# Four pre-activation layers on one core: the last image's layer 3 in another order, with one step for all norms' roots, lent buffers and evictions on either engine

## The chip, the cores and the metric

The kernel runs on one core of a Trainium2 chip. The metric is the device time of one execution in microseconds, the median of three runs. The core has TensorE (PE, matmul; PEld, its weight loads), VectorE (DVE), ScalarE (ACT), GpSimd (POOL, unused here but for a few memsets) and SyncE (SP), whose queue issues all DMAs.

## What is computed

Eight images of 32 channels and 256x256 pixels go through four layers. Each layer is `x = x + conv(gn(x))`, with a group norm over pairs of channels that needs the whole image first.

```
x = x + L0(gn(x))   # 1x1 conv; then each channel convolved with its own 5x5 pooled map
x = x + L1(gn(x))   # quantised: out = -sum |patch - w| over 32 channels x 3x3, for 32 outputs
x = x + L2(gn(x))   # 3x3 conv plus bias
x = x + L3(gn(x))   # on 8x8 windows:
#   y = layernorm(windows)
#   a = kan1(y in one 16-wide order);  d = kan2(y in another);  e = kan3(y, 32 channels)
#   out = kan4(a + d + e) + windows
# kan(v): b_k = exp(-((layernorm(v) - g_k) / denom)**2), k = 0..7
#         result = sum_k W_k b_k + W silu(v)
```

## The kernel before, in words

**Tiles.** An image of layer 3 is cut in eight units (NCH = 8) of 128 partitions x 2048 float32 (F). A unit's matmuls are 32x32 blocks: a *group* (mm16, L593) is 16 program matmuls of 512 columns, which the trace shows as 32, and it fills the PSUM tile psB (128x2048) or, in halves of eight, the tile psA (128x1024).

**Planner.** Nothing is issued in the order of the code. Every step is a task with an engine, an assumed duration, buffers and a rank (`Plan.add`). `Plan.run` simulates the four engines with these durations, picks the ready task of lowest rank whose buffers are free, and writes down the order; the engines then run this fixed order. `LAT` is the assumed hand-over from one engine to another. Buffers have kinds: `bas` (3 places for kan bases), `si` (3), `rs` (2, roots), `dv` (3 places of 128x4128 bf16, distances of layer 1), `psA`, `psB` (one each), `psV` (2, variances), and `sb`, pieces of a large arena.

**Layer 1** is not made of tasks but of *passes* (`Pass`), which fill what is left: VectorE, or in halves ScalarE, makes a clipped difference (L977, L979) into a `dv` buffer (in the first image a `bas` one also), and TensorE gathers it into psA with eight matmuls (L999). A pass ends with an eviction of psA (L1046). There are 16 passes for an image and 36 distances for each.

**Images overlap.** While layer 1 of image b runs, layer 0 of image b+1 and layers 2 and 3 of image b-1 run beside it. When the last pass of image 7 is over, only the rest of layer 3 of image 6 and layers 2 and 3 of image 7 are left, with nothing beside them: this is what is called the last image here.

**Layer 3.** A *kan* is, for a unit: scale the centred values by the roots (matmul L1264, multiply L1272 on VectorE), eight bases (a square on ScalarE, L1368, or, once layer 1 is over, a product on VectorE instead, L1374; then an exp, L1381, on ScalarE), eight groups into psB, a group of the silu, others that are added, and one eviction (L1447, or L1449 for the last kan). The kans are numbered 0 to 3 in the code, 0 being kan1 of the reference; 4 is the first layernorm. Before a kan stands `variance`: centre with a matmul (L593 into psB, in the last image in two halves into psA), evict (L1219), square (L1224), sum with a matmul into psV (L1232). `roots` makes Ln and Exp (L1245, L1249) of a psV. Exp and Ln share one table of ScalarE, silu (L1313, L1479) needs another; a change costs a table load (L1554). The planner keeps table stretches in the order in which they were added.

Results move between the layouts by DMA: y, yd and their silus are stored and read again (prepare, L1324 and L1326; L1345, L1348), so are the results oa and od of kans 0 and 1 (L1463), which kan 2 adds (load2: four DMAs for oa, L1405, sixteen for od, L1409).

**The order of a turn** is written in the last loop of `stage3`. Turn t runs kan 0 of unit t, kan 3 of unit t-1, kan 1 and kan 2 of unit t, and prepares unit t+1 and the first norm of unit t+2. Roots are made at three places of a turn, "A" (kan 0 and the next first norm), "B" (kans 1 and 3) and "C" (kan 2).

Of the kernel before, what the change touches and what calls it, by code (L numbers as in the profile page):

```python
# [89 lines left out]
class Buf:  # L90


    def __init__(self, kind, words=0):
        self.kind, self.words = kind, words
        self.writers, self.readers = [], []
        self.tile = None
        self.left, self.first, self.at, self.taken, self.base = 0, None, None, False, kind == "bas"
        self.spill = False
# [6 lines left out]
class Plan:  # L105
# [4 lines left out]
    LAT = {"PE": 0.15, "DVE": 0.12, "ACT": 0.25, "SP": 2.0}  # L110

    def __init__(self, room):
# [9 lines left out]
        self.first_pass = 0  # L122
# [40 lines left out]
    def fits(self, need, spare):  # L163
# [3 lines left out]
        for b in need:  # L167
            if b.kind in ("dv", "bas") and b.spill:
                b.kind = "dv" if self.places["dv"] else "bas"
            if b.base:  # L170
                b.kind = "bas" if self.places["bas"] else "sb"
                spare = BASE_SPARE
            if b.kind in self.places and not self.places[b.kind]:
# [17 lines left out]
    def bases_full(self):  # L191
        return not self.places["bas"] and sum(n for _, n in self.free["sb"]) < F + BASE_SPARE
# [35 lines left out]
    def run(self):  # L228
# [23 lines left out]
        while left or any(not p.done for p in self.passes):  # L252
            moved = True
            while moved:
                moved = False
                for e in engines:
# [3 lines left out]
                    if best is None:  # L260
                        for t in ready[e]:
# [4 lines left out]
                            if t.eng != e and not all(p.done for p in self.passes[self.first_pass :]):  # L266
# [5 lines left out]
                        if best is not None:  # L272
                            ready[best.eng].remove(best)
                            if best.other:
                                ready[best.other[0]].remove(best)
                                if best.eng != e:
                                    self.sets[best.stretch][1] -= 1
# [8 lines left out]
                    t.load = None  # L286
                    if t.table in (LN_EXP, SILU):
# [55 lines left out]
    def slack(self, p):  # L343
        return p.b == 0 or self.now - self.idle > IDLE

# [19 lines left out]
class Pass:  # L365
# [38 lines left out]
    def on_pe(self, plan, urgent):  # L404
# [5 lines left out]
        if self.sums and len(self.queue) < URGENT and (late or not (urgent or self.queue)):  # L410
            t, us, bufs, n = self.sums.pop(0), 0.53, [], 1
            fn = lambda: self.parts.gather(self, None, None, t)
        elif self.queue and (len(self.queue) >= URGENT or not urgent):
            o, t, d = self.queue.pop(0)
            us, bufs, n = 0.53, [d], 1
# [21 lines left out]
def kernel(  # L437
# [142 lines left out]
    def sb(b, n=None):  # L580
        return b.tile[:, : n or b.words] if b.tile is not None else arena[:, b.at : b.at + (n or b.words)]
# [588 lines left out]
    def stage3(b, norm, x3buf, rank, span):  # L1170
# [26 lines left out]
        stat = {(k, t): (Buf("psV"), Buf("rs")) for t in range(-2, U + 2) for k in "ABC"}  # L1197
# [6 lines left out]
        def parts():  # L1204

            if b < nb - 1:
# [3 lines left out]
        def variance(n, t, cen, bias, rk, src, sq=None):  # L1210
# [3 lines left out]
            for p, ps, i, us in parts():  # L1214
                at = slice(i * FS, (i + (2 if us < 1 else 4)) * FS)
                plan.add("PE", 0.85 + 0.2 * us, lambda ps=ps, i=i: cen(ps(), i), r=src, w=[p], acc=[c], rank=rk, spare=SPARE)
                plan.add(
# [6 lines left out]
            plan.add("ACT", 1.9, lambda: nc.scalar.activation(sb(sq), sb(c), AF.Square), r=[c], w=[sq], rank=rk)  # L1224
            v = stat[t][0]
# [52 lines left out]
        def front(t, after, rk):  # L1278
# [6 lines left out]
            st[t]["c4"] = variance(4, ("A", t - 1), cen, cb, rk, [xt, sm["cenf"], sm["c3"]], xt)  # L1285

        def middle(t):

            rk = turn(t - 1.0)
            y, yd = st[t]["c4"], Buf("sb", F)  # L1290
            scale(4, ("A", t - 1), y, rk)
# [17 lines left out]
        def silus(t):  # L1309
            rk = turn(t - 0.9)  # L1310
# [363 lines left out]
```

## Time and profile before

| what | us |
|---|---|
| median of three runs | 15973.13 (15972.1 to 15999.17) |
| the profiled execution | 15969.78 |
| its span, first to last instruction | 15967.3 |
| last eviction of a layer-1 pass (L1046) starts | 14601.76 |
| first and last eviction of layer 2, last image (L1145) start | 14725.80, 14837.18 |
| first eviction of layer 3, last image (L1219) starts | 14851.12 |
| evictions of kan 2 (L1447), units 1 and 6, last image, start | 15158.52, 15801.13 |
| last eviction (L1449) starts | 15956.57 |

Over the whole span PE is busy 12928.0 us (81%), DVE 13454.6 (84%), ACT 12386.4 (78%), and POOL 16.7. The kernel has no one bound: until 14601.8 VectorE and ScalarE are both nearly full, after that the engines wait for each other. The table's last lines cut out five whole turns of layer 3, from one eviction of kan 2 to the fifth after it. A busy PE in the profile is not a PE at its peak, since matmuls overlap.

### The profile page before, as it was taken

How to read it: one execution, taken by the hardware profiler on the slowest of the kernel's cores; microseconds unless marked ns; L12 is line 12 of the kernel's file. 1: busy time of each engine (PE TensorE's matmuls, PEld its weight loads, DVE VectorE, ACT ScalarE, POOL GpSimd, SP SyncE). 2: the span in 40 equal slices, each digit the busy share in tenths (PEclk: the TensorE clock that was granted, in tenths of full speed). 3: DMA queues.
4: the chain of work that ended last, by engine and by line, in shares of the span. 5: the costliest groups of instructions: out<-in, count | busy, mean ns of one | idle time of the engine just before them, and what ended most of it. 6: DMA issues, size and time to landing. Idle time of an engine off the chain costs nothing. (4 is left out here: it accounts for less than half of the span.)

```text
span 15967.3 us, 560619 instructions
## 1 busy us (share of the span) xinstructions
PE 12928.0 (81%) x260296; PEld 4325.8 (27%) x260296; DVE 13454.6 (84%) x12544; ACT 12386.4 (78%) x6843; POOL 16.7 (0%) x25
## 2 busy tenths in 40 slices
PE   5889887987887888788887888788878888877666
PEld 4333322222332222232222222222222222222222
DVE  2889889898878889888999988999898989897465
ACT  0899749678658766866888987899779987997687
POOL 0000000000000000000000000000000000000000
PEclk8989899999999999899999999899999999998777
DMA  4332446445445444643554454444544454444554
GB/s 117 78 96 54 105 113 169 109 107 153 130 101 152 126 112 120 166 106 105 152 132 123 126 134 122 122 123 127 127 126 126 126 122 138 116 132 114 144 154 130
DMA packets 1192870, 1970.85 MB, mean 123 GB/s; under 512 B 362752, under 2 KB 878848, under 8 KB 1092224
## 3 DMA queue, kind: packets, MB, share of 16 engines
q1 hardware_dynamic: 1190528, 1934.98, 46.1%
q8 instruction: 2036, 33.36, 0.9%
q14 instruction: 306, 2.51, 0.1%
HBM read 1162.83 MB, written 771.75 MB: 121 GB/s over the span
## 5 line engine op out<-in xcount | busy, mean ns | idle before, releaser
L977 DVE TENSOR_SCALAR dv<-qh,w1q 128x4128 bf16<-128x4128 bf16 (+1 forms) x8831 | 10521.9, 1248 | 1376.3 <-PE psA L999 1319.3
L999 PE MATMUL psA<-dv,sel_b 128*32 128x512 bf16 x71240 | 5434.0, 405 | 1339.6 <-DVE dv L977 1054.2
L999 PEld LDWEIGHTS <-sel_b 128*32 128x32 bf16 x82944 | 2053.9, 97 | 6792.6 <-issue 5786.5
L1368 ACT ACTIVATE bas<-arena,kb 128x2048 f32<-128x2048 f32 x1386 | 2762.3, 1993 | 408.3 <-DVE arena L1272 262.9
L1381 ACT ACTIVATE bas<-bas 128x2048 f32<-128x2048 f32 x1386 | 2653.1, 1914 | 39.0
L979 ACT ACTIVATE dv<-qh,w1n 128x2064 bf16<-128x2064 bf16 x827 | 1628.6, 2009 | 1126.8 <-PE psA L999 1035.3
L593 PE MATMUL psB<-bas,tl 32*32 32x512 f32 x48416 | 1955.5, 652 | 491.1 <-ACT bas L1381 247.6
L873 PE MATMUL psB<-arena,wt 32*32 32x512 f32 (+1 forms) x51040 | 1848.5, 607 | 99.5 <-issue 61.4
L593 PE MATMUL psB<-arena,tl 32*32 32x512 f32 x22496 | 909.4, 621 | 161.7 <-ACT si L1449 46.1
L593 PEld LDWEIGHTS psB<-bas,tl 32*32 32x32 f32 x48416 | 535.2, 107 | 1384.3 <-ACT bas L1381 518.8
L873 PEld LDWEIGHTS psB<-arena,wt 32*32 32x32 f32 x51040 | 651.2, 104 | 778.1 <-issue 607.1
L1368 ACT ACTIVATE arena<-arena,kb 128x2048 f32<-128x2048 f32 x410 | 816.1, 1991 | 0.0
L1381 ACT ACTIVATE arena<-arena 128x2048 f32<-128x2048 f32 x410 | 785.0, 1915 | 12.3
L624 DVE BATCH_NORM_STATS2 tiny<-arena 128x6 f32<-128x512 f32 x768 | 473.5, 679 | 351.8 <-ACT arena L906 246.0
L999 PE MATMUL psA<-qh,sel_b 128*32 128x512 bf16 x9216 | 672.2, 393 | 92.3 <-DMA qh<-q 77.9
L1447 ACT ACTIVATE si<-psB,cols_sb 128x2048 f32<-128x2048 f32 x192 | 377.4, 1966 | 453.3 <-PE psB L593 369.9
L1272 DVE TENSOR_TENSOR arena<-psB,arena 128x2048 f32<-128x2048 f32 x280 | 640.5, 2287 | 86.2 <-PE psB L1264 79.2
L593 PE MATMUL psB<-si,tl 32*32 32x512 f32 x14080 | 630.6, 624 | 48.8 <-ACT si L1447 19.5
L1129 PE MATMUL psB<-arena,tl 32*32 32x512 f32 (+3 forms) x16384 | 626.6, 608 | 14.7 <-issue 14.4
L1224 ACT ACTIVATE arena<-arena 128x2048 f32<-128x2048 f32 x320 | 612.7, 1915 | 15.7 <-DMA x<-arena 5.8
L1264 PE MATMUL psB<-rs,tl 32*32 32x512 f32 x8960 | 338.9, 630 | 222.5 <-DVE arena L1272 128.2
L906 ACT ACTIVATE arena<-psB,cc 128x2048 f32<-128x2048 f32 x64 | 125.7, 1964 | 493.2 <-PE psB L894 493.2
(151 smaller groups left out, 7686.6 us busy)
## 6 DMA issues: line engine op xcount, KB each, us to landing
arena<-x SPq DMA_DIRECT2D x128, 1024.0 KB
arena<-y SPq DMA_DIRECT2D x128, 1024.0 KB
si<-sy SPq DMA_DIRECT2D x512, 256.0 KB
arena<-in_x_dram SPq DMA_DIRECT2D x240, 384.0 KB
arena<-in_x_dram SPq DMA_DIRECT2D x256, 256.0 KB
x<-arena SPq DMA_DIRECT2D x256, 256.0 KB
xr<-x SPq DMA_DIRECT2D x512, 128.0 KB
x<-xr SPq DMA_DIRECT2D x512, 128.0 KB
```

What stands on the lines that cost most here:

```text
L593: nc.tensor.matmul(o[j * C : (j + 1) * C, i - first, :], w_, src(rows, i, j), start=start, stop=stop)
L624: nc.vector.bn_stats(self.stats[:, at + i, :], a[:, i * 512 : (i + 1) * 512])
L873: nc.tensor.matmul(o[:, lo - 2 * j : hi - 2 * j, c0:c1], wt[rows, t, :], d[rows, lo + dy + 2 : hi + dy + 2, c0 + dx : c1 + dx], start=firs ...
L977: nc.vector.tensor_scalar(dst, src, w1q[:, at : at + 1], 0.0, ALU.subtract, ALU.max)
L979: nc.scalar.activation(dst, src, AF.Relu, bias=w1n[:, at : at + 1])
L999: nc.tensor.matmul(psA[j * C : (j + 1) * C, i, :], sel_b[:, n, :], src[:, at : at + 2, t % 3 : t % 3 + W], **flags,)
L1129: nc.tensor.matmul(o[:, lo - 2 * j : hi - 2 * j, c0:c1], (wc if t == 4 else tl[:, W2T + t, :])[rows], d[rows, lo + dy + 1 : hi + dy + 1, c ...
L1224: plan.add("ACT", 1.9, lambda: nc.scalar.activation(sb(sq), sb(c), AF.Square), r=[c], w=[sq], rank=rk)
L1272: lambda ps=ps, at=at: nc.vector.tensor_tensor(sb(c)[:, at], ps().rearrange("p s f -> p (s f)"), sb(c)[:, at], ALU.mult),
L1368: lambda k=k, bas=bas: nc.scalar.activation(sb(bas), sb(rb), AF.Square, bias=kb[:, n, k : k + 1]),
L1381: lambda k=k, bas=bas, square=square: nc.scalar.activation(sb(bas), sb(bas), AF.Exp, scale=-1.0, bias=0.0 if square.eng == "ACT" else kbsq ...
L1447: nc.scalar.activation(sb(o), psB.rearrange("p s f -> p (s f)"), AF.Identity, bias=obias)
```

## The change

The durations that the planner assumes are changed: LAT, the gather (0.53 to 0.49), and 0.05 more for TensorE when it changes between a gather and another task. The rest works only in the last image, or once all passes are over (`over()`):

- bases may lie in `dv` places, and `si` tiles too (a new flag `side`), when their own places are full;
- the half evictions of `variance` and its square may run on VectorE instead of ScalarE, whichever is free first;
- the turn is `alone(t)` instead of `beside(t)` (the old order): one psV and one pair of roots for four norms of the turn, for unit t's kans 1 and 2, unit t+1's kan 0, unit t+2's first norm and unit t-1's kan 3. Kans run in the order 1, 2, 3, 0, and units run one turn further ahead;
- kan 2's loads of oa and od wait for its first exp instead of its fifth.

```diff
-    LAT = {"PE": 0.15, "DVE": 0.12, "ACT": 0.25, "SP": 2.0}
+    LAT = {"PE": 0.2, "DVE": 0.15, "ACT": 0.3, "SP": 2.0}
...
             if b.base:
-                b.kind = "bas" if self.places["bas"] else "sb"
+                b.kind = "bas" if self.places["bas"] else "dv" if self.over() and self.places["dv"] else "sb"
                 spare = BASE_SPARE
+            if b.side:
+                b.kind = "si" if self.places["si"] or not self.over() else "dv" if self.places["dv"] else "sb"
...
-                            if t.eng != e and not all(p.done for p in self.passes[self.first_pass :]):
+                            if t.eng != e and not self.over():
                                 continue
...
+                    if e == "PE":
+                        us += 0.05 * ((t.n is None) != self.filling)
+                        self.filling = t.n is None
...
+    def over(self):
+        return all(p.done for p in self.passes[self.first_pass :])
...
-            t, us, bufs, n = self.sums.pop(0), 0.53, [], 1
+            t, us, bufs, n = self.sums.pop(0), 0.49, [], 1
...
-            us, bufs, n = 0.53, [d], 1
+            us, bufs, n = 0.49, [d], 1
...
-                plan.add(
+                evict = plan.add(
                     "ACT", 0.15 + 1.8 * us,
...
-            plan.add("ACT", 1.9, lambda: nc.scalar.activation(sb(sq), sb(c), AF.Square), r=[c], w=[sq], rank=rk)
-            v = stat[t][0]
+                evict.other = "DVE", 0.15 + 2.1 * us, lambda ps=ps, at=at: nc.vector.tensor_scalar(
+                    sb(c)[:, at], ps().rearrange("p s f -> p (s f)"), shift, None, ALU.add
+                )
+            square = plan.add("ACT", 1.9, lambda: nc.scalar.activation(sb(sq), sb(c), AF.Square), r=[c], w=[sq], rank=rk)
+            square.other = "DVE", 2.3, lambda: nc.vector.tensor_tensor(sb(sq), sb(c), sb(c), ALU.mult)
+            v = stat.setdefault(t, (Buf("psV"), Buf("rs")))[0]
...
-                        "SP", 2.0 if name == "oa" else 8.0, load2, r=[db], w=[a], rank=rk, after=exps[4:5], spare=F,
+                        "SP", 2.0 if name == "oa" else 8.0, load2, r=[db], w=[a], rank=rk, after=exps[(0 if last else 4) :][:1], spare=F,
...
+        def alone(t):
+
+            now, nxt, old = 0 <= t < U, 0 <= t + 1 < U, 1 <= t
+            if now:
+                prepare(1, t, t, turn(t - 0.6), exp0(2, t - 1))
+            if t + 2 < U:
+                front(t + 2, t, turn(t - 0.5), exp0(2, t - 1) or (st[t + 1]["y"].writers if nxt else []))
+            if now:
+                prepare(2, t, t, turn(t - 0.4), exp0(2, t - 1))
+            if nxt:
+                prepare(0, t + 1, t, turn(t - 0.2), exp0(3, t - 2))
+            if old:
+                prepare(3, t - 1, t, turn(t - 0.3), [])
+            roots(t, turn(t))
+            if now:
+                kan(1, t, t, turn(t + 0.05))
+            if t + 2 < U:
+                middle(t + 2, t, turn(t))
+            if old:
+                silu_z(t - 1, turn(t + 0.1))
+            if t + 2 < U:
+                silus(t + 2, turn(t + 0.1))
+            if now:
+                kan(2, t, t, turn(t + 0.25))
+            if old:
+                kan(3, t - 1, t, turn(t + 0.5))
+            if nxt:
+                kan(0, t + 1, t, turn(t + 0.75))
+
+        for t in range(-2, U + 1):
+            (alone if last else beside)(t)
```

`prepare`, `front`, `middle`, `silus` and `silu_z` take the turn's psV and the rank as arguments now; what they do is the same. `exp0(n, t)` is the first exp of kan n of unit t.

## The prediction, made before the changed kernel was run

> **What bounds the kernel now.** I read the busy time by stretches first, then the costliest groups, and then, for the last image's layer 3, ScalarE's and TensorE's order of time. The columns of the stretch table are the stretch and its length, then busy us (with instructions) of PE, PEld, DVE, ACT and POOL, then the granted clock, the DMA share and GB/s.
>
> ```profile
> 12000.00:14000.00 2000.00, 1643.85 (x30910) 509.08 (x30908) 1806.72 (x1520) 1757.74 (x975) 3.89 (x2) 0.92 0.48 127
> ...
> 14601.80:14725.80 124.00, 79.00 (x1686) 34.43 (x1686) 70.00 (x61) 87.82 (x48) 0.00 (x0) 0.78 0.51 120
> ...
> 14851.10:14939.60 88.50, 40.53 (x504) 7.75 (x504) 26.06 (x16) 42.16 (x29) 0.00 (x0) 0.60 0.38 131
> 14939.60:15158.50 218.90, 145.67 (x2520) 49.57 (x2520) 134.74 (x69) 186.11 (x116) 0.00 (x0) 0.76 0.56 150
> 15158.50:15801.10 642.60, 432.19 (x7968) 154.42 (x7968) 401.38 (x203) 536.70 (x324) 0.00 (x0) 0.77 0.56 155
> 15801.10:15967.30 166.20, 102.01 (x1856) 28.65 (x1856) 73.50 (x36) 112.18 (x67) 0.00 (x0) 0.76 0.36 96
> ```
>
> Two kernels stand here one behind the other. Up to 14601.8, where the last gather of layer 1 is evicted, VectorE makes distances and is 90% busy, ScalarE 88%. After it only the last image is left, and no engine is full: between 15158.5 and 15801.1 five whole turns of layer 3 take 128.5 us each, of which ScalarE works 536.7/5 = 107.3 and stands idle 21.2, while VectorE works 80.3.
>
> ```profile
> L977 DVE TENSOR_SCALAR dv<-qh,w1q 128x4128 bf16<-128x4128 bf16 (+1 forms) x8831 | 10521.9, 1248 | 1376.3 <-PE psA L999 1319.3
> ```
>
> Nearly all of VectorE's idle time in the long part is a wait for TensorE to give back one of three distance buffers. The idle time of a turn looks like this:
>
> ```profile
> 15047.43 1.02 ACT L1219 ACTIVATE arena<-psA 128x1024 f32<-128x1024 f32 x1 [2.12 <-PE psA L593]
> ...
> 15054.37 1.02 ACT L1219 ACTIVATE arena<-psA 128x1024 f32<-128x1024 f32 x1 [2.78 <-PE psA L593]
> 15055.43 1.91 ACT L1224 ACTIVATE arena<-arena 128x2048 f32<-128x2048 f32 x1
> 15059.39 0.69 ACT L1245 ACTIVATE rs<-psV,eps_c 128x512 f32<-128x512 f32 x1 [2.06 <-PE psV L1232]
> ```
>
> The reader sees ScalarE and TensorE taking turns on the one half-tile psA, each waiting for the other: a norm's chain with nothing beside it. TensorE's part of it costs twice as much there:
>
> ```profile
> 15060.79 1.96 PE L1264 MATMUL psA<-rs,tl 32*32 32x512 f32 x16 [1.47 <-ACT rs L1249]
> 15064.21 1.96 PE L1264 MATMUL psA<-rs,tl 32*32 32x512 f32 x16 [1.45 <-DVE arena L1272]
> ```
>
> The granted clock is 0.58 between 15040 and 15075 and 0.91 between 15075 and 15100.
>
> **The change, part by part. Work in a turn.** By the built order of the changed program a whole turn has 57 ScalarE instructions where it had 65. Five half evictions (1.02, L1219) and three squares (1.91, L1224) go to VectorE, two of three pairs of roots (0.69 + 0.63) go, and four more basis squares come back from VectorE (2.00, L1368): -5.1 - 5.7 - 2.6 + 8.0 = -5.4, so 101.9 us. VectorE loses four products (2.35, L1374), and gets five half evictions and three squares. No row has these two on VectorE. The eviction lies between 0.65 (half of L1294, 1.29 for 2048 from SBUF) and 1.22 (L1272, 1024 from PSUM); I take 1.22, the row that also reads PSUM. The square lies between 1.29 and 2.35; I take 2.29, L1272's two tensors. That is -9.4 + 6.1 + 6.9 = +3.6, so 84 us: VectorE stays below ScalarE. The Trainium skill (VectorE: DVE Perf Modes, "Why PSUM operands drop a tier") says that float32 read from PSUM gets no faster mode; by it the eviction is 1.22, and the sum stays. The table loads (two of 1.28 a turn) and the DMAs (52 a turn, the 16 of od that hold SP's queue for 11.5 us among them) are as many as before. POOL is not touched.
>
> **The path through a turn**, hand over hand along the built order, from the roots' Ln at 0. Roots 1.4; two scale steps of 1.96 + 1.22 and hand-overs, 3.4 each as between the two L1264 lines: 8.1. Norm 1's kan: three squares and eight exps at 1.90 (the spacing of back-to-back ones), 1.7 lost because the first product stands behind a third scale step on VectorE: 31. Table load, silu of z, eviction, two silus, load: 41. Kan 2, nine instructions: 58. Seven instructions of kan 3, then the eviction of kan 2: 73. The od load has landed by about 63 (stored at 36, 6.3 to land, gate at kan 2's first exp, 11.5 of issue), so it is hidden; the next turn's loads behind it on SP land by 70 and are wanted at 75. Two matmul groups of kan 3 must free a buffer (1.32 each, 10.8 us for eight in the chain), then four ScalarE instructions and a square: 86. Five evictions, one square and five exps between the centring steps, 16.7, with some 1.3 of waiting: 104. Kan 3's eviction 3.99: 108. Again two groups, 2.6; then kan 0's last groups, which TensorE runs one after the other (six at 1.32, one centring step 1.1, three at 1.15): 121. Eviction: 123. ScalarE's idle time is still about 21: the roots' wait at the start is longer (6.7), the rest smaller pieces. So a turn is 123 instead of 128.5. Bounds: 119, where the eviction is 0.65 and every step between groups runs at the high clock; 128, where five more half steps cost 1.96 instead of 1.1.
>
> The Trainium skill (TensorE: Matmul & The Clock Gate, "What's actually happening") has the array at half clock after an idle window of about 3.4 us and at full clock after as long a busy one. TensorE idles 3.3 us over eviction and roots, so by this rule the first steps of each turn stay slow, as I have them; were they fast, a turn would be 121. The rule also speaks against putting all norms behind one eviction.
>
> **The layer from its first norm to the end.** The first turn now centres four tensors (yd, y, y, x3) ahead of the second roots where it centred two: two more pairs of steps of 3.2 each, 12.7; with the loads waited for anyway the roots come 12 later, y's scale steps stand before kan 0's and cost 3.5 more, eviction by VectorE 1 to 2. First kan's eviction ends at 14956 instead of 14939.6: +16.5. From there: 95 for the turn without kan 3, five of 123, 117 for the one without a front (silus of y 3.7 and two evictions less), 95 for the last with three kans, 41 for the last kan alone (15926.02 to the end, as before): 963. Before it was 15967.3 - 14939.6 = 1027.7. So -65 + 16.5 = -48.
>
> **The end of image 6.** In the stretch from 14601.8 the old order still has four kan evictions and 29 exps of image 6, the new one three and 22: a kan's rest has moved ahead of the last gather. The next kan eviction comes at about +27 instead of +48 (14650.01): -20 here. What hides it there is ScalarE's and VectorE's idle tenth; if that cover is gone it comes back as 20. Layer 2 of the last image (14725.8 to 14851.1) has the same instructions: 0.
>
> **Planner costs.** They touch all 14,600 us before. Distances per engine stay (VectorE two whole ones more and three halves less, ScalarE three halves less), the order changes almost from the start. The new costs of TensorE are the trace's: groups and gathers in alternation repeat every 1.62 (new 1.03 + 0.49 + 0.10, old 1.56), gathers in a row every 0.49 (old 0.53).
>
> ```profile
> 10025.77 1.15 PE L593 MATMUL psB<-arena,tl 32*32 32x512 f32 x32
> ...
> 10027.39 1.14 PE L593 MATMUL psB<-arena,tl 32*32 32x512 f32 x32
> ```
>
> The new hand-over of 0.20 from TensorE is longer than the trace's (a gather's 0.62 from 10023.17 ends 0.05 before VectorE starts at 10023.84). What the order is worth no row shows; bounds are a tenth of the 1319.3 either way, -130 to +130, and I take 0, with 45 of spread.
>
> **Sum.** 15967.3 - 48 - 20 = 15899; the profiled run took 2.5 more than its span (15969.78), and the median of the runs, 15973.13, is 3.3 above that run: 15905.
>
> **Rivals.** *The order of the long part gets better too*: VectorE's wait for TensorE falls by a tenth, 130; 15905 - 130 = 15775, or half of it, 15840. For it: costs that now meet the trace, and 50 fewer changes to and fro on TensorE. *It stays where it is*: ScalarE's 21 us of idle become 26 and a turn stays at 128, +30, and the 20 come back: 15955. For it: 65 to 57 instructions saves only 5.4 us a turn, and neither engine was full. *Slower*: in the long part TensorE's order holds VectorE up. Runs of six or more groups between two gathers are 40 where they were 34, with 930 more program matmuls in them, 930/16 x 1.15 = 67 us in which three buffers (3.7 us of distances) soon run out. It decides from a growth of L977's wait by 100 us (7.6% of 1319.3); at the bound, 130: 15905 + 130 = 16035. *The lent buffers are not used*: the built order has 85 VectorE products into dv tiles, so this falls.
>
> **How the numbers follow.** Forecast 0.50, better 0.15, stays 0.22, slower 0.13. The forecast's own range is 15865 to 15940 (turns of 119 to 128, five and a half of them: -22 and +28, and part of the order's spread); the range 15835 to 15985 takes in the half of the better case and the staying one. About 0.2% (32 us) is what a measurement tells from no change, so faster is below 15941: 0.50 + 0.15 = 0.65, same 0.22, slower 0.13.
>
> **What would show it.** Steps right: the last layer-1 eviction within 40 us of 14601.8, whole turns of 123, ScalarE's work per turn 102, two root instructions per turn, VectorE's eviction at 1.22. Wrong: turns of 128 or below 117, or a shift of the last gather by more than 45, which is the order's and which I cannot derive.

## The result, and the profile after

The changed kernel takes 16034.31 us (median of six runs, 16021.0 to 16042.22), the kernel before 15973.65 beside it: a ratio of 1.0033, with an interval of 1.002 to 1.0045. The profiled execution took 16032.62, its span is 16030.5, 63.2 above the span before. From here on a time in a table is the one at which an instruction ends.

| where, us | before | after | later by |
|---|---|---|---|
| last eviction of a layer-1 pass | 14602.9 | 14674.3 | 71.5 |
| first eviction of layer 2, last image | 14727.8 | 14787.6 | 59.8 |
| last eviction of layer 2 | 14839.1 | 14897.5 | 58.4 |
| first eviction of a kan in layer 3 | 14939.6 | 15029.5 | 89.9 |
| end | 15967.3 | 16030.5 | 63.2 |

So nearly all of the loss is there before layer 3 of the last image, which was to become shorter, begins; and layer 3 loses 31.5 up to its first kan and wins 26.7 from there on. New lines: L593 of before is L605 of after, L977 is L989, L999 is L1011, L1219 is L1232 (on VectorE L1237), L1224 is L1240 (L1241), L1232 is L1249, L1245 is L1262, L1249 is L1266, L1264 is L1281, L1272 is L1289, L1313 is L1328, L1368 is L1383, L1381 is L1396, L1447 is L1462. In the other kernels they lie a few lines further up or down; the operation and the tiles tell which is meant.

The busy time of after by stretches, with the columns of the prediction's table (stretch and length, then PE, PEld, DVE, ACT and POOL, granted clock, DMA share, GB/s):

```profile
12000.00:14000.00 2000.00, 1632.34 (x30868) 508.84 (x30858) 1805.06 (x1522) 1747.42 (x968) 5.24 (x3) 0.94 0.48 126
14673.20:14785.60 112.40, 65.06 (x1358) 31.85 (x1358) 57.03 (x55) 64.50 (x37) 0.00 (x0) 0.73 0.47 114
14897.50:15030.30 132.80, 63.77 (x670) 13.29 (x670) 67.05 (x67) 36.63 (x26) 0.00 (x0) 0.59 0.38 135
15139.20:15772.80 633.60, 445.75 (x8064) 152.10 (x8064) 420.48 (x225) 506.79 (x284) 0.00 (x0) 0.81 0.58 157
15772.80:16030.50 257.70, 150.22 (x2944) 50.51 (x2944) 155.04 (x79) 184.01 (x101) 0.00 (x0) 0.76 0.44 111
```

The fourth row holds five whole turns, from roots to roots: 126.7 each, ScalarE busy 101.4 and idle 25.4, VectorE busy 84.1. The work is what was forecast (101.9 and 84); the idle time is not (21). The long part, in the costliest groups of after:

```profile
L989 DVE TENSOR_SCALAR dv<-qh,w1q 128x4128 bf16<-128x4128 bf16 (+1 forms) x8815 | 10496.8, 1248 | 1496.5 <-PE psA L1011 1429.5 <-issue 27.2 <-ACT dv L991 11.4
```

VectorE's work is the same, and its wait for TensorE's gathers has grown from 1319.3 to 1429.5, by 110.2. Part of that has only moved there from another row, that of the distances which the first image makes into `bas` places; before, then after:

```profile
L977 DVE TENSOR_SCALAR bas<-qh,w1q 128x4128 bf16<-128x4128 bf16 (+1 forms) x309 | 317.0, 1041 | 37.1 <-PE psA L999 37.1
L989 DVE TENSOR_SCALAR bas<-qh,w1q 128x4128 bf16<-128x4128 bf16 (+1 forms) x324 | 351.3, 1094 | 0.0
```

Over both rows the wait has grown from 1356.4 to 1429.5, by 73.1, which is the size of the 71.5 by which the last pass ends later. The loss does not build up evenly: the last passes of the eight images end later by 1.6, 79.4, 8.0, 39.3, 84.8, 77.3, 66.8 and 71.5, so the third image gives nearly all back that the second loses.

In layer 3 of the last image (from layer 2's last eviction to the end) ScalarE's busy time falls from 877.2 to 798.0, its idle time rises from 251.0 to 335.0: 79 us of work were taken away, and 84 us of waiting came. The groups of ScalarE over that stretch say where; before, then after:

```profile
L1368 ACT ACTIVATE bas<-arena,kb 128x2048 f32<-128x2048 f32 x26 | 51.9, 1997 | 36.0 <-DVE arena L1272 32.3 <-PE psB L593 2.9 <-ACT bas L1381 0.8
L1245 ACT ACTIVATE rs<-psV,eps_c 128x512 f32<-128x512 f32 x26 | 17.6, 675 | 21.1 <-PE psV L1232 21.1
```

```profile
L1383 ACT ACTIVATE bas<-arena,kb 128x2048 f32<-128x2048 f32 x36 | 71.9, 1998 | 103.1 <-DVE arena L1289 78.8 <-PE psB L605 20.0 <-issue 4.2
L1262 ACT ACTIVATE rs<-psV,eps_c 128x512 f32<-128x512 f32 x11 | 7.5, 683 | 50.5 <-PE psV L1249 50.5
```

Fifteen pairs of roots fewer, and yet the wait ahead of the roots has more than doubled (21.1 to 50.5), as has the wait of a kan's first square for the scaled norm (32.3 to 78.8). A turn of after, all engines, in order of time (TensorE's weight loads and SP left out):

```profile
15265.30 1.97 ACT L1462 ACTIVATE si<-psB,cols_sb 128x2048 f32<-128x2048 f32 x1 [2.53 <-PE psB L605]
15265.83 1.06 PE L1249 MATMUL psV<-arena,tl 128*32 128x512 f32 x8 [0.57 <-DVE arena L1241]
15267.16 0.68 ACT L1262 ACTIVATE rs<-psV,eps_c 128x512 f32<-128x512 f32 x1
15267.87 0.63 ACT L1266 ACTIVATE rs<-rs 128x512 f32<-128x512 f32 x1
15268.56 1.09 PE L1281 MATMUL psA<-rs,tl 32*32 32x512 f32 x16 [1.66 <-ACT rs L1266]
...
15271.03 1.96 PE L1281 MATMUL psA<-rs,tl 32*32 32x512 f32 x16 [1.39 <-DVE arena L1289]
...
15274.38 1.96 PE L1281 MATMUL psA<-rs,tl 32*32 32x512 f32 x16 [1.38 <-DVE arena L1289]
15276.44 1.23 DVE L1289 TENSOR_TENSOR arena<-psA,arena 128x1024 f32<-128x1024 f32 x1 [2.12 <-PE psA L1281]
15277.70 2.00 ACT L1383 ACTIVATE bas<-arena,kb 128x2048 f32<-128x2048 f32 x1 [9.20 <-DVE arena L1289]
```

Kan 0 is evicted, and with it ScalarE has nothing left: it makes the roots and then stands idle for 9.2 us, while three scale steps go back and forth between TensorE and VectorE.

### The profile page after: what moved, and what is told of

Its sections match the earlier page's. It is cut to its first block, busy times and chain, and to the rows that moved or that the text cites. A ratio compares the mean times of both kernels' runs of the same rounds, so it can differ in the third digit from the quotient of the medians.

```text
span 16030.5 us, 560619 instructions
## 1 busy us (share of the span) xinstructions
PE 12954.8 (81%) x260296; PEld 4332.4 (27%) x260296; DVE 13514.1 (84%) x12595; ACT 12313.4 (77%) x6762; POOL 25.9 (0%) x25
## 5 line engine op out<-in xcount | busy, mean ns | idle before, releaser
L989 DVE TENSOR_SCALAR dv<-qh,w1q 128x4128 bf16<-128x4128 bf16 (+1 forms) x8815 | 10496.8, 1248 | 1496.5 <-PE psA L1011 1429.5
L1011 PE MATMUL psA<-dv,sel_b 128*32 128x512 bf16 x71048 | 5427.4, 405 | 1377.1 <-DVE dv L989 1111.2
L1011 PEld LDWEIGHTS <-sel_b 128*32 128x32 bf16 x82944 | 2051.5, 97 | 6818.7 <-issue 5812.6
L1383 ACT ACTIVATE bas<-arena,kb 128x2048 f32<-128x2048 f32 x1412 | 2814.4, 1993 | 492.4 <-DVE arena L1289 305.4
L1396 ACT ACTIVATE bas<-bas 128x2048 f32<-128x2048 f32 x1412 | 2703.2, 1914 | 40.6
L605 PE MATMUL psB<-bas,tl 32*32 32x512 f32 x48128 | 1935.4, 653 | 493.4 <-ACT bas L1396 240.2
L605 PE MATMUL psB<-arena,tl 32*32 32x512 f32 x19648 | 809.8, 626 | 130.6 <-ACT si L1464 46.6
L605 PEld LDWEIGHTS psB<-bas,tl 32*32 32x32 f32 x48128 | 524.5, 107 | 1377.2 <-issue 504.8
L1383 ACT ACTIVATE arena<-arena,kb 128x2048 f32<-128x2048 f32 x401 | 798.2, 1991 | 0.0
L1396 ACT ACTIVATE arena<-arena 128x2048 f32<-128x2048 f32 x401 | 767.8, 1915 | 11.6
L1011 PE MATMUL psA<-qh,sel_b 128*32 128x512 bf16 x9216 | 669.2, 396 | 92.6 <-DMA qh<-q 77.0
L1289 DVE TENSOR_TENSOR arena<-psB,arena 128x2048 f32<-128x2048 f32 x280 | 640.2, 2286 | 87.1 <-PE psB L1281 76.4
L605 PE MATMUL psB<-si,tl 32*32 32x512 f32 x13888 | 612.5, 624 | 42.1 <-DVE arena L1289 13.1
L1141 PE MATMUL psB<-arena,tl 32*32 32x510 f32 (+3 forms) x16384 | 630.7, 613 | 17.0 <-issue 16.4
L1462 ACT ACTIVATE si<-psB,cols_sb 128x2048 f32<-128x2048 f32 x191 | 375.0, 1964 | 350.6 <-PE psB L605 308.7
L1240 ACT ACTIVATE arena<-arena 128x2048 f32<-128x2048 f32 x290 | 555.2, 1914 | 8.7
L1281 PE MATMUL psB<-rs,tl 32*32 32x512 f32 x8960 | 350.2, 652 | 215.5 <-DVE arena L1289 124.1
```

The source lines that it names most:

```text
L605: nc.tensor.matmul(o[j * C : (j + 1) * C, i - first, :], w_, src(rows, i, j), start=start, stop=stop)
L989: nc.vector.tensor_scalar(dst, src, w1q[:, at : at + 1], 0.0, ALU.subtract, ALU.max)
L1011: nc.tensor.matmul(psA[j * C : (j + 1) * C, i, :], sel_b[:, n, :], src[:, at : at + 2, t % 3 : t % 3 + W], **flags,)
L1141: nc.tensor.matmul(o[:, lo - 2 * j : hi - 2 * j, c0:c1], (wc if t == 4 else tl[:, W2T + t, :])[rows], d[rows, lo + dy + 1 : hi + dy + 1, c ...
L1240: square = plan.add("ACT", 1.9, lambda: nc.scalar.activation(sb(sq), sb(c), AF.Square), r=[c], w=[sq], rank=rk)
L1289: lambda ps=ps, at=at: nc.vector.tensor_tensor(sb(c)[:, at], ps().rearrange("p s f -> p (s f)"), sb(c)[:, at], ALU.mult),
```

## The experiments

One profile of each kernel was taken, besides timed runs. How far one profile can be trusted shows in kernels that share an order. Eleven of those below have the same order in the long part (old costs), and their last layer-1 eviction ends between 14602.9 and 14634.4. Before's own is the earliest of them, so a shift against it can look up to 31.5 too large. Layer 3 of the last image repeats better: in the four with its old code and the old hand-over costs (before, e4, s2, s3) it takes 1124.7 to 1128.1. "Two-engine" means that half evictions and centred squares may go to VectorE, "loan" the buffers of layer 1 lent to layer 3, "costs" the planner's.

| kernel | last layer-1 eviction | first of layer 2 | layer 3 | ratio to before (interval) |
|---|---|---|---|---|
| before | 14602.9 | 14727.8 | 1128.1 | |
| after | 14674.3 | 14787.6 | 1133.0 | 1.0033 (1.002, 1.0045) |
| e1 old costs | 14613.3 | 14747.0 | 1148.6 | 1.002 (1.0011, 1.0029) |
| e2 new costs alone | 14679.7 | 14782.5 | 1139.7 | 1.0026 (1.0015, 1.0036) |
| e3 hand-over costs alone | 14597.4 | 14766.8 | 1135.4 | 1.0039 (1.0024, 1.0054) |
| e4 gather and switch costs alone | 14665.9 | 14770.7 | 1124.7 | 1.003 (1.0018, 1.0041) |
| s2 a piece's cost + 0.01 | 14713.5 | 14758.8 | 1126.2 | 1.0014 (1.0005, 1.0023) |
| s3 a gather's cost + 0.005 | 14556.0 | 14726.6 | 1127.2 | 1.0009 (1.0, 1.0019) |
| e5 e1, old order | 14605.9 | 14740.2 | 1104.8 | 0.9992 (0.9982, 1.0001) |
| e6 e1, no loan | 14634.4 | 14760.2 | 1117.4 | 0.9995 (0.9985, 1.0005) |
| e7 e1, no two-engine | 14610.6 | 14744.5 | 1176.0 | 1.0036 (1.0025, 1.0047) |
| p1 e1, first norms held | 14618.7 | 14753.9 | 1141.9 | 1.0018 (1.0009, 1.0027) |
| q1 old order, two-engine alone | 14608.0 | 14731.9 | 1125.2 | 1.0 (0.9991, 1.0009) |
| q2 old order, then new, no loan | 14623.8 | 14751.2 | 1117.4 | 0.9993 (0.9984, 1.0002) |
| r1 e5, loan for the last image alone | 14619.9 | 14747.6 | 1105.7 | 0.9993 (0.9984, 1.0002) |
| r2 e5, no two-engine | 14616.5 | 14749.1 | 1185.3 | 1.0044 (1.003, 1.0058) |
| r3 e1, kan 0 held behind the roots | 14614.3 | 14749.0 | 1153.3 | 1.002 (1.001, 1.0029) |

### Which part moved the long part: e1, e2

e1 is after with the costs of before, e2 is before with the costs of after. e2's edit:

```diff
-    LAT = {"PE": 0.15, "DVE": 0.12, "ACT": 0.25, "SP": 2.0}
+    LAT = {"PE": 0.2, "DVE": 0.15, "ACT": 0.3, "SP": 2.0}
...
+                    if e == "PE":
+                        us += 0.05 * ((t.n is None) != self.filling)
+                        self.filling = t.n is None
...
-            t, us, bufs, n = self.sums.pop(0), 0.53, [], 1
+            t, us, bufs, n = self.sums.pop(0), 0.49, [], 1
...
```

> The changed kernel with the planner's old costs (LAT 0.15/0.12/0.25, 0.53 a gather, no 0.05 for a switch); layer 3 of the last image in its new order, the loan and the two-engine evictions stay. Theory 'order': the new costs alone made the long part longer by reordering it, so the last eviction of layer 1 (before 14601.8, after 14673.2 us) returns to 14602 within 3, and what follows it (before 1365.5, after 1357.3 us) stays near 1357: a span of 15957 to 15962 and a ratio to before of 0.999 to 1.000. Rival 'the new end disturbs the long part': the last eviction of layer 1 stays near 14673 and the span near 16030, ratio 1.004. Mixed: between the two.

> The kernel before with nothing but the planner's new costs. Theory 'order': the last eviction of layer 1 at 14673 within 3 and before's 1365.5 us behind it, so a span of 16036 to 16041 and a ratio to before of 1.004 to 1.005, and the wait of VectorE's squared sums for psA near 1422 us where before has 1312. Rival 'the new end disturbs the long part': last eviction near 14602, span near 15967, ratio 1.000.

The place came out as the theory "order" says: with old costs the last layer-1 eviction is back (14613.3, not within the 3 us expected, but within what one order repeats to), with the new costs alone it is 76.8 late. VectorE's wait in e2, by the costliest groups:

```profile
L980 DVE TENSOR_SCALAR dv<-qh,w1q 128x4128 bf16<-128x4128 bf16 (+1 forms) x8815 | 10497.2, 1248 | 1496.3 <-PE psA L1002 1425.5 <-issue 32.8 <-ACT dv L982 10.2
```

Its 1425.5 is after's 1429.5, without any other part of the change. The whole time is less clear than the place: e2's timed runs are 46 us above before's in the median, a ratio of 1.0026 where 1.004 to 1.005 was expected, and its profiled run (16031.25) was the slowest of eight. What the theory had wrong is the rest: e1's span is 16004.7, not 15957 to 15962, since the rest of image 6 took 133.7 where after has 113.2, and layer 3 1148.6 where after has 1133.0. In the median e1 is 33 us slower than before without any new cost. The part behind the long one has to be explained by itself.

### Size of a cost, or a new deal: e3, e4, s2, s3

> The kernel before with the new hand-over costs alone (LAT 0.2/0.15/0.3). If one of the new costs is to blame by its size and it is this one: last eviction of layer 1 near 14673, ratio 1.0045. If it is the other: near 14602, ratio 1.000. If any new cost deals the order of the long part afresh and what comes out is luck: anywhere within 80 us of 14602, on either side, and this one's shift and the other's don't add up to the 71.4 us of both together.

> The kernel before with the new gather cost (0.49 for 0.53) and the 0.05 for a switch between groups and gathers, the hand-over costs as they were. If one of the new costs is to blame by its size and it is this one: last eviction of layer 1 near 14673, ratio 1.0045. If it is the other: near 14602, ratio 1.000. If the order is luck: anywhere within 80 us of 14602, on either side, and the shifts of the two runs don't add up to 71.4.

e3 has the LAT line of the diff above alone, e4 the rest of it. The last layer-1 eviction moves by -5.5 and +63.0, which add up to 57.5 where both together moved it by 76.8, a difference that the repeat of 31.5 covers. That looks as if the gather's cost were to blame; but e3, whose eviction hardly moves, has the worst ratio of the four, because the rest of image 6 then takes 169.5 us instead of 124.9, and layer 2 130.7 instead of 111.4. Two kernels with a meaningless step of a cost:

```diff
# s2
-        us = (0.05 + 1.24 * (hi - lo) / RH) if e == "DVE" else 0.2 + 3.54 * (hi - lo) / RH
+        us = (0.06 + 1.24 * (hi - lo) / RH) if e == "DVE" else 0.2 + 3.54 * (hi - lo) / RH
# s3
-            t, us, bufs, n = self.sums.pop(0), 0.53, [], 1
+            t, us, bufs, n = self.sums.pop(0), 0.535, [], 1
...
```

> The kernel before with one planner cost moved by 0.01 us: what each of VectorE's distance pieces costs beside its length, 0.06 for 0.05. Nothing real stands behind it. Theory 'a new deal': the order changes from early on and layer 2's first eviction of the last image lies anywhere from 20 below to 80 us above before's 14727.8, as with e3 (+39) and e4 (+43), where the costs were moved four to five times as far. Rival 'the size of the cost decides': it stays within 10 us, ratio 1.000.

> The kernel before with the planner's cost of a gather moved by 0.005 us, away from the trace's 0.49: 0.535 for 0.53. Theory 'a new deal': layer 2's first eviction anywhere from 20 below to 80 us above 14727.8. Rival 'the size of the cost decides': within 10 us, and if anything the other way from e4's, which moved the same cost to 0.49.

A hundredth of a microsecond in an assumed duration moves the last layer-1 eviction by +110.6, five thousandths by -46.9. VectorE's wait follows, s2 and then s3:

```profile
L977 DVE TENSOR_SCALAR dv<-qh,w1q 128x4128 bf16<-128x4128 bf16 (+1 forms) x8813 | 10507.8, 1250 | 1475.0 <-PE psA L999 1411.5 <-issue 25.0 <-ACT dv L979 9.0
```

```profile
L977 DVE TENSOR_SCALAR dv<-qh,w1q 128x4128 bf16<-128x4128 bf16 (+1 forms) x8835 | 10516.1, 1247 | 1348.1 <-PE psA L999 1304.8 <-issue 8.9 <-ACT dv L979 6.1
```

So steps of a cost as small as these two deal the order anew. How late each order is against before depends on where one looks; the last line has the kernels with before's order and no loan in image 6 (q1, q2, r1, e6), the last column the medians of the timed runs:

| order, us later than before | last layer-1 eviction | first of layer 2 | last of layer 2 | timed |
|---|---|---|---|---|
| e2 | +76.8 | +54.7 | +50.4 | +46 |
| e3 | -5.5 | +39.0 | +58.5 | +60 |
| e4 | +63.0 | +42.9 | +37.9 | +47 |
| s2 | +110.6 | +31.0 | +25.6 | +17 |
| s3 | -46.9 | -1.2 | +16.9 | +16 |
| before's, again | +5.1 to +31.5 | +4.1 to +32.4 | +3.8 to +31.1 | |

The reader should see that the last layer-1 eviction is a poor mark: behind it s2 has only 45.3 us of image 6 left, s3 has 170.6. What the layer-1 passes gain, image 6 can lose. The first eviction of layer 2, which the expectations name, is not the best mark either: by it s3 would be its rival's, but in s3 and e3 a last kan of image 6 still runs beside layer 2, which takes 129.3 and 130.7 where before has 111.4. By the last eviction of layer 2 all five are late, s2 and s3 within the repeat, and all five are slower in the timed runs, with s3's interval reaching 1. None is better than before's. Why before's order stands at the good end of six is open; that it had been kept as the best of several would do it, and no run here tells.

The mechanism that the prediction's rival named, long runs of groups on TensorE during which the three buffers run out, fits but isn't proved. Counted in the traces (a group is 32 matmuls there), TensorE's matmuls that stand in runs of 84 or more between two gathers are 26614 (s3), 27554 (e3), 28266 (before), 30848 (e4), 31854 (after) and 35344 (s2), in the order of VectorE's waits over both rows of distances (1328.5, 1347.4, 1356.4, 1373.5, 1429.5, 1435.1). With runs of 112 or more the two no longer go together (after 25308, s2 23580), and no kernel shortened the runs alone.

### Layer 3: order, loan, two-engine steps (e5, e6, e7)

All three stand on e1, so that the long part is before's. Edits: e5 calls the old order for the last image; e6 takes the loan out; e7 takes the alternatives on VectorE out.

```diff
# e5
-            (alone if last else beside)(t)
+            beside(t)
# e6
-                b.kind = "bas" if self.places["bas"] else "dv" if self.over() and self.places["dv"] else "sb"
+                b.kind = "bas" if self.places["bas"] else "sb"
...
-            if b.side:
-                b.kind = "si" if self.places["si"] or not self.over() else "dv" if self.places["dv"] else "sb"
...
# e7
-                evict.other = "DVE", 0.15 + 2.1 * us, lambda ps=ps, at=at: nc.vector.tensor_scalar(
...
-            square.other = "DVE", 2.3, lambda: nc.vector.tensor_tensor(sb(sq), sb(c), sb(c), ALU.mult)
```

> As e1 (the planner's old costs), but the last image's layer 3 in the old order, with its three pairs of roots a turn; only the loan of layer 1's buffers and the evictions and squares on either engine are kept. Theory 'prologue': layer 3 in the new order is 25 to 30 us shorter from its first kan eviction on (1001 and 1017 us in the two profiles that have it, against 1024 to 1039 in the four that have the old) and 31.5 us longer ahead of it (132 against 100.5), so that the order as a whole is worth nothing; here the first kan eviction comes at 100 to 104 us behind layer 2's last eviction, and layer 3 takes 1105 to 1135, with the part behind the first kan eviction at 1005 to 1035. Rival 'the loan or the two-engine evictions cost': layer 3 takes 1140 to 1150 as in e1.

> As e1, without the loan of layer 1's distance buffers to the last image's layer 3; new order and two-engine evictions stay. If the loan is what lets the new order run: the bases run out of buffers ahead of each joint pair of roots and a turn grows by several of the 1.9 us exps, layer 3 from 1149 (e1) to 1170 or more, ScalarE's idle time growing by as much. If the loan is worth nothing: 1139 to 1159 as in e1.

> As e1, with every half eviction and every centred square of the last image back on ScalarE; new order and loan stay. If ScalarE's work sets the turn: five halves (1.02) and three squares (1.91) come back to it, +10.8 us a turn less what basis squares go to VectorE for it, so layer 3 from 1149 (e1) to 1170 to 1200. If the turn is set by the chain through TensorE and what ScalarE is given fills its idle time: within 10 us of e1's 1149.

e5 takes 1104.8: 43.8 us less than e1, by the order alone, and below the layer 3 of before and of after. Its first kan is evicted 102.5 behind layer 2. So at old costs, with the loan, the new order does not break even but loses, and 29 of it lie ahead of the first kan, where "prologue" put all of the loss. e7 hits its first branch: 27 us more with the work back on ScalarE. e6 missed both of its theories: without the loan the new order is 31 us *shorter*. Its turns are 124.2 (the five whole ones, 621.1) against 129.3 in e1. ScalarE at the start of one of them:

```profile
15235.96 0.69 ACT L1257 ACTIVATE rs<-psV,eps_c 128x512 f32<-128x512 f32 x1 [2.03 <-PE psV L1244]
15236.69 0.63 ACT L1261 ACTIVATE rs<-rs 128x512 f32<-128x512 f32 x1
15237.22 1.99 ACT L1391 ACTIVATE bas<-bas,kbsq 128x2048 f32<-128x2048 f32 x1
15241.65 1.97 ACT L1457 ACTIVATE si<-psB,cols_sb 128x2048 f32<-128x2048 f32 x1 [2.44 <-PE psB L600]
15243.83 2.01 ACT L1378 ACTIVATE bas<-arena,kb 128x2048 f32<-128x2048 f32 x1 [0.21 <-DVE arena L1284]
```

Short of buffers, kan 0's last exp and its eviction (L1457) come behind the roots, the scale steps run beside them, and the first square follows with 0.21 of waiting where after had 9.20. The lent buffers let kan 0 finish early and leave the roots bare. Whether that is what makes the turns longer these two views don't show; r3, below, tests it.

### The start of the layer: p1

```diff
-                prepare(1, t, t, turn(t - 0.6), exp0(2, t - 1))
+                prepare(1, t, t, turn(t - 0.6), exp0(2, t - 1) or exp0(0, t))
...
-                prepare(2, t, t, turn(t - 0.4), exp0(2, t - 1))
+                prepare(2, t, t, turn(t - 0.4), exp0(2, t - 1) or exp0(0, t))
```

> As e1, with one thing changed: the two norms of the first turn that the new order centres ahead of the first kan are held until that kan's first exp, as all later ones are. Theory 'prologue': the 31.5 us that the first kan's eviction comes later (132 against 100.5) are the two norms centred ahead of the second roots, with the silus that stand behind them; the second roots come 12 us earlier, the first kan's eviction at 105 to 120 behind layer 2's last eviction, and layer 3 takes 1122 to 1138 where e1 has 1149. Rival: the two norms are only moved behind the first kan, where the third roots wait for them, and nothing is won: first kan eviction earlier, layer 3 at 1142 to 1152.

The second roots did come 13.6 earlier, and the third then took 61.6 instead of 51.2; the first kan's eviction moved from 131.8 to 129.4, the layer from 1148.6 to 1141.9. The rival holds but for a rest of 7 us. After's start, ScalarE in order of time, shows what stands there besides:

```profile
14918.64 0.69 ACT L1262 ACTIVATE rs<-psV,eps_c 128x512 f32<-128x512 f32 x1 [21.11 <-PE psV L1249]
...
14978.92 0.69 ACT L1262 ACTIVATE rs<-psV,eps_c 128x512 f32<-128x512 f32 x1 [17.68 <-PE psV L1249]
...
14995.57 1.91 ACT L1328 ACTIVATE arena<-arena 128x2048 f32<-128x2048 f32 x1 [14.00 <-issue]
...
15001.27 2.00 ACT L1383 ACTIVATE bas<-arena,kb 128x2048 f32<-128x2048 f32 x1
...
15027.55 1.97 ACT L1462 ACTIVATE si<-psB,cols_sb 128x2048 f32<-128x2048 f32 x1 [4.35 <-PE psB L605]
```

Behind the second roots the new order puts the silus of unit 1 (L1328) ahead of kan 0's first square, as they stand in the order of the code: the square starts 22.4 behind the roots. Before, it started 11.5 behind them:

```profile
14904.70 0.69 ACT L1245 ACTIVATE rs<-psV,eps_c 128x512 f32<-128x512 f32 x1 [0.76 <-PE psV L1232]
...
14916.22 2.00 ACT L1368 ACTIVATE bas<-arena,kb 128x2048 f32<-128x2048 f32 x1 [10.18 <-DVE arena L1272]
```

### Is there a better mix: q1, q2, r1, r2

q1 has e5's order and no loan; q2 the old order for the first turn and the new one from the second, without the loan; r1 keeps e5's loan from image 6; r2 is e5 without the two-engine steps.

```diff
# q2
+            (alone if last and t > 0 else beside)(t)
+            if last and t == 0:
+                kan(0, 1, ("A", 1), turn(0.75))
+                middle(2, ("A", 1), turn(0.8))
+                silus(2, turn(0.85))
# r1 (and the flag set for the last image's bases and si tiles)
-                b.kind = "bas" if self.places["bas"] else "dv" if self.over() and self.places["dv"] else "sb"
+                b.kind = "bas" if self.places["bas"] else "dv" if b.lend and self.over() and self.places["dv"] else "sb"
...
```

> As e5 (old costs, old order, evictions and squares on either engine), but without the loan of layer 1's buffers: the two-engine evictions are the only part of the change that is left. Theory 'only these help': the stretch from the last gather to layer 2's first eviction goes back to 125 us (134 in the four runs with old costs and the loan), layer 3 takes 1095 to 1112 where before has 1128.1, and the time is 20 to 35 us below before, ratio 0.9978 to 0.9988. Rival 'the loan carries e5's layer 3': 1125 to 1140 and ratio 1.000.

> Old costs, no loan, two-engine evictions; the last image's layer 3 starts in the old order and goes over to the new one, with one pair of roots a turn, behind its first whole set of norms. Theory 'the new order loses at the start of the layer, and its turns are a little better': turns of 124 as in e6, the first kan's eviction 100 to 104 behind layer 2's last, layer 3 1080 to 1105, below q1 by 0 to 20. Rival 'the new order is worse in its end too, or the change of order costs a turn's wait': layer 3 1105 to 1130, above q1.

> As e5 (old costs, old order, two-engine evictions, loan), with the loan kept to the last image: the rest of image 6 gets no lent buffers. Theory 'the loan costs 9 us in the rest of image 6 and gains 20 in the last image's layer 3 in its old order': from the last gather to layer 2's first eviction 124 to 127 us (134 in e5), layer 3 at 1102 to 1108, the profiled part behind the last gather 1335 to 1345 (before 1364.4), ratio to before 0.9980 to 0.9990. Rival 'what the rest of image 6 gains, layer 3 gives back': layer 3 at 1115 or more, ratio 0.9992 or more.

> As e5, without the two-engine evictions and squares: the old order with the loan alone. If the loan is what makes layer 3 short in the old order (e5 1104.8 with it, q1 1125.2 without): 1105 to 1115. If it needs ScalarE to have the time for it, which only the two-engine evictions give: 1122 to 1135, near before's 1128.

q1: the stretch behind the last gather is 124.0 as expected, but layer 3 is 1125.2, the rival's: two-engine steps by themselves win 2.9 us, no more than the 3.4 within which layer 3 repeats. r2 missed both theories by 50 us: the loan by itself costs 57. Both together win 23 (e5, and r1's 1105.7). Layer 3, at old costs:

| | neither | two-engine | loan | both |
|---|---|---|---|---|
| old order | 1128.1 | 1125.2 | 1185.3 | 1104.8 |
| new order | not tried | 1117.4 | 1176.0 | 1148.6 |

No part has a price of its own: the loan is worth +57, -20 and +31 to the layer according to what it meets, the two-engine steps -2.9 and, with the loan, -80.5 in the old order and -27.4 in the new. r2's group of first squares shows it by the same wait as e6 and after did:

```profile
L1376 ACT ACTIVATE bas<-arena,kb 128x2048 f32<-128x2048 f32 x25 | 50.0, 1999 | 80.4 <-DVE arena L1282 80.4
```

80.4 us of waiting for a scaled norm, where before has 32.3. r1 takes 127.7 for the rest of image 6 (134.3 with the loan there, in e5) and keeps the layer at 1105.7, so the two do come apart, but the ratio that its theory gave did not come: 0.9993, with 1 inside the interval. q2 was 12.4 us over the top of its expected layer (1117.4), and 7.8 below q1. q2 and r1 are 8 and 16 us below before in the medians, and no kernel tried is faster beyond doubt.

### Does cover for the roots help: r3

```diff
-            roots(t, turn(t))
+            root = roots(t, turn(t))
...
+                for held in st[t]["exps0"][6:] if t else []:
+                    root.outs.append(held)
+                    held.wait += 1
...
```

> As e1 (new order, loan, old costs), with the last two exps of each kan 0 from the second turn on held until the joint roots are done. Theory 'the loan takes away the roots' cover': with the loan a kan 0 has buffers for all its bases, is done and evicted ahead of the roots, and ScalarE then waits 8.7 us a turn for the first scaled norm (52.0 in the five turns of e1 under that wait, 15.0 in e6, where a last exp and the eviction stand behind the roots). Here that wait falls below 30 and a turn of e1's 129.4 to 122 to 127, layer 3 from 1149 to 1120 to 1138. Rival 'the wait only moves': the eviction of kan 0 behind the roots holds TensorE's next kan up instead, and a turn stays at 128 to 131.

ScalarE's groups in the five turns, e1 and then r3:

```profile
L1380 ACT ACTIVATE bas<-arena,kb 128x2048 f32<-128x2048 f32 x26 | 51.9, 1997 | 65.0 <-DVE arena L1286 43.5 <-PE psB L602 17.2 <-issue 4.2
L1259 ACT ACTIVATE rs<-psV,eps_c 128x512 f32<-128x512 f32 x6 | 4.1, 687 | 15.1 <-PE psV L1246 15.1
```

```profile
L1393 ACT ACTIVATE bas<-bas,kbsq 128x2048 f32<-128x2048 f32 x59 | 117.6, 1993 | 24.7 <-DVE bas L1386 24.7
L1380 ACT ACTIVATE bas<-arena,kb 128x2048 f32<-128x2048 f32 x16 | 32.0, 2002 | 37.6 <-PE psB L602 21.5 <-DVE arena L1286 16.0
L1259 ACT ACTIVATE rs<-psV,eps_c 128x512 f32<-128x512 f32 x5 | 3.4, 688 | 39.0 <-PE psV L1246 39.0
```

The wait for the scaled norm fell from 43.5 to 16.0, as meant, and the time went to the roots' wait for the variances (15.1 to 39.0) and to exps that wait for VectorE's products (nothing to 24.7). A turn is 130.2, not the 122 to 127 that was expected, and the layer 1153.3. The rival's verdict, though at another place than it named: the wait moved. So in e1 ScalarE's missing cover is a symptom, not what sets the turn, and why the loan lengthens the new order's turns stays open. The runs don't tell which loop of norms, kans and buffers sets a turn of 124 to 130.

## Why the prediction was wrong

**Planner costs: the step that failed first.** "What the order is worth no row shows; bounds are ... -130 to +130, and I take 0, with 45 of spread." With the new costs alone (e2) layer 2's first eviction came 54.7 later in the profile, and in after 59.8 of the 63.2 stand there; in e2's timed runs the costs are worth +46, of which 11.6 lie in layer 3. The bounds held the result; the value 0 and the narrow spread didn't. The rival "slower" named this place and its test, a growth of L977's wait by 100 us: the row that it read grew by 110.2, both rows of distances by 73.1. What was missing is the view that s2 and s3 give: this order, made by simulation, turns on steps of a constant that mean nothing, and a re-deal of it spreads over +17 to +59 at layer 2's last eviction, with 31 of repeat. Costs "that now meet the trace" were no argument for a better order, nor 50 fewer changes to and fro.

**Layer 3: the second, -48 forecast, +4.9 measured.** The work was right, as shown above; VectorE's half eviction takes 1.22 and its square 2.29 (L1241), as taken. The places where the chain was too short, by the same parts:

- First kan's eviction: +16.5 forecast, +31.5 measured. The second roots come 15.8 later, for which 12 was taken (p1 shows 13.6 of it to be the two norms centred ahead); what stands between them and kan 0's first square, taken as 3.5 more for y's scale steps, cost 10.8, since the silus of unit 1 stand there too; kan 0 itself took 4.8 more.
- Turn without kan 3: 109.7 for 95. Whole turns: 126.7 for 123 each, 18.5 in all, of which 2.4, in four of the five turns, is the first square at 10.5 behind the roots' Ln instead of 8.1, since three scale steps and not two stand ahead of it. The rest was not taken apart; ScalarE's wait for TensorE's groups into psB, ahead of evictions and squares, is 56.9 in the five turns, where before's has 36.9.
- The last three parts: 112.1 for 117, 103.0 for 95, 42.6 for 41.

From the first kan on this makes 1001 for 963. Common to them, as far as the runs go, is an assumption: that work taken off ScalarE shortens a chain on which it waits for a sixth of the time. By itself the work moved by the two-engine steps was worth 2.9 (q1). The rival "stays" said so ("21 us of idle become 26"; measured 25.4), and it was right for this part.

**End of image 6: right for the costs, too large for the whole.** -20 forecast, -11.7 measured. With the costs alone it is 102.9, -22.0 (e2). The loan takes 8 to 10 back: at old costs the stretch is 132.7 to 135.2 in the six kernels with the loan there and 124.0 to 127.7 in the five without. Nor is this a gain apart from the planner costs, as the sum had it: what is left of image 6 at the last gather is what the order has put off, as s2 (110.6 late, 45.3 left) and s3 (46.9 early, 170.6 left) show.

**Layer 2:** 0 forecast, -1.5 measured. **Clock:** in four of the five turns the first scale step behind the roots is fast in after (1.09) and the next are slow (1.96 each, with 1.4 us between them); the prediction had all of them slow. It took 3.3 us for TensorE's idle time there; the turn shown above has 0.57 and 1.66, with 1.06 of matmuls between them. The Trainium skill (TensorE: Matmul & The Clock Gate, "What's actually happening") gives half clock after an idle window of about 3.4 us. The 3.3 falls just short of that, and the fast first step agrees with it. The slow second one shows that the window need not be idle throughout: from 15266.91 to 15270.32 the granted clock is 1.00 and TensorE works 1.09 of the 3.41 us, and from 15270.32 on the clock is 0.50. How much work in such a window would have kept the clock up, no run was made to tell.

With the long part as it was (e1) the kernel is still 33 us slower than before in the median; had layer 3 won its 48, the new costs' 46 (e2) would have eaten them. Both steps had to be right.

## What to carry to other kernels

Where a planner writes the order, a change of its constants is a new deal for the whole program: price it by what small meaningless steps of a constant do, and time it apart from the change it comes with. Work taken off an engine that is partly idle in a chain can come back as waiting, as 79 us of it did here; ask of every helper (a loan, another engine) what cover it takes away. And parts of such a change don't add up: the same loan was worth +57 and -20.

## What was not expected of the hardware

The whole time of the kernel before spreads by 0.3% on one chip (15956.97 to 16005.13 in 33 runs), while layer 3 of the last image repeats within 3.4 us in the profiles of four kernels that share it, so that a profile of the stretch told apart what the times couldn't.
